# Cross-attention of a decoder layer: context sums behind the keys' norms, normed rows spread over a sequence, first queries turned before two value products

## The chip, the cores and the metric

The kernel runs on one core of one Trainium2 chip. The metric is the device time of one execution in microseconds (us); lower is better. The program's instructions are put into one queue for each engine ahead of time, by a planner that works with its own estimate of every duration; on the chip each queue runs in order, and an instruction starts when it is at the head of its queue and what it waits for has happened. Engine names in the profile: PE multiplies matrices (PEld loads its weights), DVE does vector work, ACT activations and copies, POOL general elementwise work, SP starts transfers.

## The reference, cut to what matters

Eight sequences of 112 tokens and width 512 pass one decoder layer: causal self-attention, cross-attention over 375 context rows for each sequence (32 heads of 16), and a mixture of eight experts (two for each token) plus a shared one. The change touches the cross-attention and the third layer norm behind it:

```python
x = x + attention(layernorm(x))
xn = layernorm(x)
q = rmsnorm((xn @ Wq.T).reshape(b, n, 32, 16))
kv = concat([ctx @ Wk.T, ctx @ Wv.T], -1).reshape(b, m, 32, 16, 2)
k, v = rmsnorm(kv[..., 0]), kv[..., 1]
x = x + softmax(q @ k.T * 16 ** -0.5) @ v
x = x + experts(layernorm(x))        # the third layer norm: xn3 in the kernel
```

## The kernel before, in words

**Stages.** Self-attention goes over four groups of heads, to about 423 us of the span. Then come the queries of all tokens and the first sequence's keys and values (423 to 482 us), then the loop of cross-attention over sequences b = 0 to 7 (482 to 742 us), and last the experts. All matrices are in 32-bit floats.

**Tokens.** They lie in seven tiles of 128 rows. Sequences 1 to 7 have the first 112 rows of a tile; sequence 0 is spread over the last 16 rows of all seven. So its queries need all seven tiles and are read with gaps.

**One pass of the loop.** For each half of the heads (`cp`) and each third of the context (`m`), `exp_scores` multiplies keys by queries (L816) into four PSUM tiles of the pool `sc`, and ACT takes the exponentials (L827). `weigh` multiplies the half that is pending by the values (L844, 96 small products). `attend(b - 2)` turns a finished tile and adds it to the rows. `produce` makes keys and values of sequence b + 1 in small portions. All other products (keys, values, `weigh`, every transpose) take their output from the pool `mm`, which has four tiles: a fifth product waits until an earlier one was read.

**Keys and values ahead.** The two first thirds of a context are multiplied with seven products in place of eight (`first_chunks`, L656). This needs four sums of context blocks, which POOL makes into the tiles `csum[0]` to `csum[3]` (`chunk_sums` and `block_sums`, L636 to L644). The first is read by the sixth product, the second by the second, the third by the fourth, the fourth by the seventh, and the result of the seventh is written to the values by DVE at L677. The third thirds of two neighbouring sequences are done together (`third_chunks`, with `pair_sums`, which writes `csum[0]`, `[1]`, `[4]` and `[2]`). So the same four tiles are written anew for every sequence. `chunk_sums(b)` is traced at the start of pass b - 1, but POOL may run it as soon as its tiles are free and its context is there; before, nothing else holds it.

**The boundary of two passes.** The squares of the last keys are made on POOL (L571) and summed on DVE (L572). `rms_scale_quick` takes reciprocal (DVE, L583) and square root (ACT, L584), with an activation table load on either side. `normed_k` (L787) then scales three thirds of the keys (DVE, L792, three instructions), turns them (PE, L797) and copies them (ACT, L800). `issue_after(last_exp[(b, 1, 2)])` puts these copies behind the last exponentials of the pass in ACT's queue. The next pass begins with an L816 product that is kept behind all that was traced on PE before it. `spread_q` (L775) makes the queries of a coming sequence in two DVE instructions (L779).

**The third layer norm.** `ln_apply` (L156) scales a tile's rows (DVE, L153, two buffers `xn`), turns them with four PE transposes (L160, output in `mm`) and copies them to `xn3` (ACT, L161). Tiles 0 to 3 are done at the boundary of passes 5 and 6, in this place:

```python
                if b == 5:
                    for t in range(4):
                        ln_apply(mv3, rs3, t, xn3)
```

They are first used in pass 7, by `shared_ahead` (L911).

**Before the loop.** Lines 890 to 899 give the order of the last steps: value product of the first third, keys of sequence 0, value product of the second third, `normed_q` of the last tile (L764: scaling, four transposes L772, copy L773), `spread_q(0)`, value product of the last third. Under `issue_after(squared)` POOL makes differences of weights (L627) and `chunk_sums(1)` beside these.

Of the kernel before, what the change touches and what calls it, by code (L numbers as in the profile page):

```python
# [18 lines left out]
ALU = mybir.AluOpType  # L19
# [57 lines left out]
def decoder_layer(  # L77
    ctx: ExitStack, tc: tile.TileContext, x, ctxT, wqk, wv_all, wo, wx, wgate, wsgu, wsd, wegu, wed_a, wed_b, consts, out
):
    nc = tc.nc  # L80
# [36 lines left out]
    def psum(pool, name):  # L117
        return pool.tile([P, 512], F32, tag=pool.name, name=name)
# [32 lines left out]
    def ln_normed(mv, rs, t):  # L151
        xn = lnpool.tile([P, D], F32, tag="xn", name="xn")
        nc.vector.tensor_scalar(xn, xs[t], mv[:, t, 0:1], rs[:, t : t + 1], ALU.subtract, ALU.mult)  # L153
        return xn

    def ln_apply(mv, rs, t, xnT):  # L156
        xn = ln_normed(mv, rs, t)
        pt = psum(mm, "ln_t")
        for c in range(ND):
            nc.tensor.transpose(pt[:, c * P : (c + 1) * P], xn[:, c * P : (c + 1) * P], ident)  # L160
        nc.scalar.copy(xnT[:, :, t * P : (t + 1) * P], pt.rearrange("p (c s) -> p c s", c=ND))  # L161
# [15 lines left out]
    with ExitStack() as sa:  # L177
# [120 lines left out]
        for g in range(NG):  # L298
# [226 lines left out]
            for i, b in enumerate(order):  # L525
# [10 lines left out]
                if b in (0, 6, 7):  # L536
                    t = max(b - 5, 0)
# [6 lines left out]
    mv3 = ln_begin("3")  # L544
    xn2 = xnpool.tile([P, ND, NT], F32, tag="xnT", name="xn2")
    xn3pool = ctx.enter_context(tc.tile_pool(name="normed3", bufs=1, side="right"))
    xn3 = xn3pool.tile([P, ND, NT], F32, name="xn3")
    with ExitStack() as xa:
# [11 lines left out]
        wxk, wxv, wxq = (load_w(wpool, wx[i], f"wx{i}") for i in range(3))  # L560
# [37 lines left out]
        def by_head(t):  # L598
            return t.rearrange("p (h d) -> p h d", h=XH)
# [15 lines left out]
        def project_v(b, m):  # L615
            nc.vector.tensor_copy(values[b % 2][:, m, :, :XD], by_head(project(b, m, wxv, "xv")))
# [12 lines left out]
        csum = [stp.tile([P, 2, MC], F32, name=f"csum{i}") for i in range(4)]  # L629
# [3 lines left out]
        def halves(b, m):  # L633
            return [ctxs[b][:, 2 * k : 2 * k + 2, m * MC : (m + 1) * MC] for k in range(2)]

        def block_sums(a11, a12, a21, a22, dst):  # L636

            nc.gpsimd.tensor_tensor(dst[0], a21, a22, ALU.add)
            nc.gpsimd.tensor_tensor(dst[1], dst[0], a11, ALU.subtract)
            nc.gpsimd.tensor_tensor(dst[2], a11, a21, ALU.subtract)  # L640
            nc.gpsimd.tensor_tensor(dst[3], a12, dst[1], ALU.subtract)

        def chunk_sums(b):
            block_sums(*halves(b, 0), *halves(b, 1), csum[:4])  # L644

        def pair_sums(b):
            block_sums(*halves(b, 2), *halves(b + 1, 2), [csum[0], csum[1], csum[4], csum[2]])
# [1 line left out]
        def product(x, w):  # L649
            ps = psum(mm, "kv")  # L650
            for c in range(2):
                nc.tensor.matmul(ps[:MC, :], x[:, c, :], w[:, c, :], start=(c == 0), stop=(c == 1))  # L652
            return ps[:MC, :]

        def first_chunks(b):

            (a11, a12), (a21, a22) = halves(b, 0), halves(b, 1)
            k0, k1 = rawk[b][0][:, 0, :], rawk[b][0][:, 1, :]
            v0, v1 = (values[b % 2][:, m, :, :XD] for m in range(2))
            u = stp.tile([MC, 512], F32, tag="u", name="u")  # L660
            nc.scalar.copy(k0, product(a11, wxk[:, 0:2]))
            yield
            nc.vector.tensor_tensor(u, product(csum[1], wt[1]), k0, ALU.add)
            yield
            nc.vector.tensor_tensor(k0, product(a12, wxk[:, 2:4]), k0, ALU.add)  # L665
            key_squares(b, 0)
            yield
            nc.vector.tensor_tensor(v1, by_head(product(csum[2], wt[2])), by_head(u), ALU.add)
            yield
            nc.vector.tensor_tensor(by_head(k1), by_head(product(a22, wt[3])), v1, ALU.add)  # L670
            key_squares(b, 1)
            yield
            p5 = product(csum[0], wt[0])
            nc.vector.tensor_tensor(v1, by_head(p5), v1, ALU.add)
            nc.vector.tensor_tensor(u, p5, u, ALU.add)
            yield
            nc.vector.tensor_tensor(v0, by_head(product(csum[3], wxv[:, 2:4])), by_head(u), ALU.add)  # L677
            yield

        def third_chunks(b):  # L680
# [32 lines left out]
        def produce(b, cp, m):  # L713

            if (cp, m) == (0, 0):
                new_keys(b)
                produce.first = first_chunks(b)
                if b > 1:
                    chunk_sums(b)
                if b + 1 < B:  # L720
                    ctxs[b + 1] = load_ctx(b + 1)
            first = produce.first
            if b == B - 1:
                if cp == 0:
                    steps(2, first)
                elif m == 0:
                    project_k(b, 2)
                elif m == 1:
                    project_v(b, 2)
                else:  # L730
                    steps(1, first)
            elif b % 2:
                if cp == 0:
                    steps(2, first)
                    if m == 2:
                        pair_sums(b)
                        produce.third = third_chunks(b)
                else:
                    if m == 1:
                        steps(1, first)  # L740
                    steps((2, 1, 2)[m], produce.third)
            else:
                if cp == 0 and m < 2:
                    steps(1, produce.third)
                steps(((0, 1, 2), (2, 1, 1))[cp][m], first)
# [29 lines left out]
        def spread_q(b):  # L775

            queries[b] = qtp.tile([P, ND, 2, S], F32, tag="qT2", name="qT2")
            for e in range(2):
                nc.vector.tensor_scalar(  # L779
                    like_seq(queries[b][:, :, e, :], b),  # L780
                    seq(xn2, b),
                    cst[:, C_EO + e : C_EO + e + 1],
                    None,
                    ALU.mult,
                )

        def normed_k(b):  # L787
            k, kss = rawk.pop(b)
            keys[b] = kvp.tile([P, ND, M], F32, tag="kT2", name="kT2")
            for m in range(NM):  # L790
                k3 = k[:, m, :].rearrange("p (h d) -> p h d", h=XH)
                nc.vector.tensor_tensor(  # L792
                    k3, k3, kss[:, m, :, None].to_broadcast([MC, XH, XD]), ALU.mult
                )
                pt = psum(mm, "kT")
                for c in range(ND):
                    nc.tensor.transpose(  # L797
                        pt[:, c * MC : (c + 1) * MC], k[:, m, c * P : (c + 1) * P], ident[:MC, :MC]
                    )
                nc.scalar.copy(  # L800
                    keys[b][:, :, m * MC : (m + 1) * MC],
                    pt[:, : ND * MC].rearrange("p (c s) -> p c s", c=ND),
                )
# [88 lines left out]
        project_v(0, 0)  # L892
        rms_scale(rawk[0][1].rearrange("p m h -> p (m h)"))
        normed_k(0)
        project_v(0, 1)
        normed_q(TT - 1)
        spread_q(0)
        project_v(0, 2)
        ctxs[1] = load_ctx(1)

# [5 lines left out]
        def shared_ahead(i, k):  # L906
# [6 lines left out]
                )  # L913
            nc.vector.tensor_copy(ahead[:, 2 * i + k, :HALF], ps[:, :HALF])

        pending = None
        for b in range(B):
            for cp in range(2):
                es = []
                for m in range(NM):  # L920
                    es.append(exp_scores(b, cp, m))
                    if m == 0 and pending is not None:
                        weigh(*pending)

                    if m == 1 and cp == 0 and b >= 2:
                        attend(b - 2)
                    if b + 1 < B:
                        produce(b + 1, cp, m)
                    elif m:
                        shared_ahead(cp, m - 1)  # L930
                pending = (b, cp, es)
            if b + 1 < B:
                spread_q(b + 1)

                with tc.issue_after(last_exp[(b, 1, 1)].ins):
                    if b == 5:
                        rs3 = ln_rstd(mv3, 0, 4)
                    rms_scale_quick(rawk[b + 1][1].rearrange("p m h -> p (m h)"))

                    tc.keep_in_program_order(nc.scalar.activation(warm, eps_rms[:1], AF.Exp))  # L940
                with tc.issue_after(last_exp[(b, 1, 2)].ins):
                    normed_k(b + 1)
                if b + 2 == B:
                    sw = [load_shared(i) for i in range(2)]
                    ahead = wpool.tile([P, 4, 512], F32, tag="w", name="ahead")
                if b == 5:
                    for t in range(4):
                        ln_apply(mv3, rs3, t, xn3)
        weigh(*pending)
        attend(TT - 1)  # L950

# [4 lines left out]
    with ExitStack() as ff:  # L956
# [190 lines left out]
        halves = (slice(0, SL), slice(SL, P))  # L1147
# [254 lines left out]
```

## Time and profile before

| what | value |
|---|---|
| median of 3 runs | 995.17 us (992.79 to 996.33) |
| the profiled execution | 994.56 us |
| its span (first to last instruction) | 992.7 us |
| granted TensorE clock, mean over the span | 0.997 |
| DVE, ACT, POOL busy | 44%, 30%, 36% of the span |

The profile shows one execution. Its span leaves 1.86 us outside. Starts are in us from the span's start. In a row of the timeline the number after the start is the duration of the whole row, and a bracket gives the idle time of the engine before it and what ended it. First products of the passes (L816) start at these times:

| pass b | 0 | 1 | 2 | 3 | 4 | 5 | 6 | 7 |
|---|---|---|---|---|---|---|---|---|
| start, us | 482.54 | 513.83 | 543.74 | 578.41 | 609.50 | 644.26 | 679.43 | 712.45 |

### The profile page before, as it was taken

To read this page: it belongs to the slowest core of one execution; us is meant where nothing else is said; L and a number is where in the kernel's file an instruction comes from. 1 tells how busy PE (TensorE), PEld (TensorE's weight loads), DVE (VectorE), ACT (ScalarE), POOL (GpSimd) and SP (SyncE) were. 2 spreads that over 40 slices of the span, in tenths; PEclk is the share of its full clock that TensorE was granted. 3 is DMA by queue.
4 is the path that set the end of the run, shared out by engine and by line. 5 is a ranking of instruction groups with operands and counts; after the bars stand their busy time and mean duration, and the time that the engine had idled before them with its cause. 6 is when DMAs were issued, how large, how long until landed. Compare 5 with 4: busy or idle time off the path is not lost.

```text
span 992.7 us, 16065 instructions
## 1 busy us (share of the span) xinstructions
PE 968.1 (98%) x6008; PEld 580.6 (58%) x6008; DVE 432.5 (44%) x885; ACT 302.7 (30%) x759; POOL 357.0 (36%) x408
## 2 busy tenths in 40 slices
PE   5999999999999999999999999999999999999998
PEld 3569756985598559845455555555665544444433
DVE  4346433542364236764445455544435143333324
ACT  3135102501151115224355355545542121111100
POOL 4337744683468444433523222321114600000023
PEclk9999999999999999999999999999999999999999
DMA  9522002201220121000010001100219648777755
GB/s 348 204 95 75 21 22 89 81 2 43 86 83 1 43 86 41 2 0 1 32 33 33 20 14 33 33 2 1 86 60 424 231 131 259 236 236 236 214 183 168
DMA packets 35324, 98.89 MB, mean 100 GB/s; under 512 B 4848, under 2 KB 10224, under 8 KB 31664
## 3 DMA queue, kind: packets, MB, share of 16 engines
q1 hardware_dynamic: 30192, 85.26, 25.7%
q0 software_dynamic: 2320, 7.63, 2.4%
q10 hardware_dynamic: 2736, 4.98, 1.7%
q8 instruction: 48, 0.79, 0.3%
q14 instruction: 28, 0.23, 0.1%
HBM read 78.85 MB, written 14.94 MB: 94 GB/s over the span
## 4 chain that ended last, share of the span: by engine, by line
PE 86%; DVE 4%; issue 4%; POOL 3%; DMA 2%; ACT 0%; POOLq 0%; SPq 0%; DVEq 0%; ACTq 0%
PE qk L274 16%; PE kv L652 12%; PE v L393 7%; PE o L473 7%; PE gu L972 5%; PE y L1230 5%; PE gate L1208 5%; PE up L1208 4%; PE xs L816 4%; PE pv L844 4%; PE z L230 3%; PE s L191 3%; PE o L432 1%; PE v L364 1%; POOL sq L571 1%
## 5 line engine op out<-in xcount | busy, mean ns | idle before, releaser
L827 ACT ACTIVATE e<-xs 125x448 f32<-125x448 f32 x192 | 88.4, 545 | 92.0 <-PE xs L816 92.0
L1241 POOL DMA_INDIRECT got<-routed,at x14 | 15.9, 1135 | 172.7 <-issue 172.4
L274 PE MATMUL qk<-xc,wc 128*128 128x448 f32 x180 | 70.1, 539 | 0.0
L652 PE MATMUL kv<-wx,ctx 128*125 128x512 f32 x120 | 56.7, 603 | 0.0
L211 ACT ACTIVATE s<-s,mx 112x112 f32<-112x112 f32 x128 | 48.1, 376 | 27.7 <-DVE mx L208 17.0
L1208 PE MATMUL gate<-wex,xT 128*64 x144 | 55.3, 466 | 0.5 <-ACT xT L1173 0.5
L972 PE MATMUL gu<-xn,sw 128*128 128x448 f32 x144 | 55.5, 541 | 0.0
L1208 PE MATMUL up<-wex,xT 128*64 x144 | 54.3, 459 | 0.0
L274 PEld LDWEIGHTS qk<-xc,wc 128*128 128x128 f32 x180 | 34.2, 190 | 33.5 <-issue 32.3
L1158 DVE COPY xn<-wex 128x704 f32 x60 | 31.2, 524 | 51.5 <-PE up L1208 51.5
L571 POOL TENSOR_TENSOR sq<-kraw 125x512 f32<-125x512 f32 x24 | 25.1, 1046 | 78.3 <-DVE kraw L665 20.5
L816 PEld LDWEIGHTS xs<-qT,kT 32*125 32x125 f32 x768 | 33.5, 183 | 32.6 <-issue 24.1
L816 PE MATMUL xs<-qT,kT 32*125 32x224 f32 x768 | 50.3, 374 | 1.5 <-DVE qT L779 1.5
L274 PE MATMUL qk<-xn,w 128*128 128x448 f32 x120 | 50.2, 539 | 0.0
L1230 PE MATMUL y<-wd,hT 128*64 128x512 f32 (+1 forms) x216 | 49.5, 592 | 0.6 <-ACT y L1234 0.6
L216 POOL TENSOR_TENSOR s<-s,sm 112x448 f32<-112x448 f32 x32 | 29.8, 932 | 49.5 <-DVE sm L215 45.0
L1208 PE MATMUL gate<-xn,xT 128*64 128x352 f32 x120 | 45.9, 464 | 0.0
L1208 PE MATMUL up<-xn,xT 128*64 128x352 f32 x120 | 45.3, 459 | 0.0
L972 PEld LDWEIGHTS gu<-xn,sw 128*128 128x128 f32 x144 | 26.8, 190 | 24.2 <-issue 24.2
L844 PE MATMUL pv<-e,v 125*32 125x112 f32 x1536 | 40.1, 260 | 0.2
L844 PEld LDWEIGHTS pv<-e,v 125*32 125x32 f32 x1536 | 36.3, 110 | 5.2 <-issue 3.2
L652 PE MATMUL kv<-wx,csum 128*125 128x512 f32 x80 | 38.9, 609 | 0.0
(274 smaller groups left out, 1965.5 us busy)
## 6 DMA issues: line engine op xcount, KB each, us to landing
wd<-in_wed_a SPq DMA_DIRECT2D x27, 512.0 KB, 3.8
wex<-in_wegu SPq DMA_DIRECT2D x8, 1408.0 KB, 19.2
wd<-in_wed_b SPq DMA_DIRECT2D x36, 192.0 KB, 4.5
w<-in_wqk SPq DMA_DIRECT2D x6, 1024.0 KB, 4.9
ctx<-in_ctxT SPq DMA_DIRECT2D x8, 750.0 KB, 4.3
slots<-zeros SPq DMA_DIRECT2D x1, 4608.0 KB, 20.0
wd<-in_wed_a SPq DMA_DIRECT2D x18, 256.0 KB, 4.4
routed<-y SPq DMA_DIRECT2D x18, 256.0 KB, 3.4
```

The source lines that it names most:

```text
L211: nc.scalar.activation(s[:, h, :], s[:, h, :], AF.Exp, bias=mx[:, h : h + 1], accum_out=sm[:, h : h + 1])
L274: nc.tensor.matmul(ps[:, :HALF], wt[:, c * P : (c + 1) * P], x[:, c, :], start=(c == 0), stop=(c == 1))
L393: nc.tensor.matmul(ps[:, :wide], x[:, c, cols], w[:, c, :], start=(c == 0), stop=(c == 1))
L473: nc.tensor.matmul(ps[:, :wide], x[:, h, :], w[:, h, :], start=(h == 0), stop=(h == 1))
L571: i = nc.gpsimd.tensor_tensor(sq[:n], dst, dst, ALU.mult)
L652: nc.tensor.matmul(ps[:MC, :], x[:, c, :], w[:, c, :], start=(c == 0), stop=(c == 1))
L816: i = nc.tensor.matmul(strips[j][:MC, ci * 2 * S : (ci + 1) * 2 * S], keys[b][rows, 2 * cp + ci, m * MC : (m + 1) * MC], queries[b][rows, ...
L827: last_exp[(b, cp, m)] = nc.scalar.activation(e[:, :, j, :, :].rearrange("p c e s -> p c (e s)"), strips[j][:MC, : 4 * S].rearrange("p (c ...
L844: nc.tensor.matmul(ps[VW * j : VW * (j + 1), g * S : (g + 1) * S], v[:, m, 16 * cp + h, :], es[m][:, h // 8, (h % 8) // 2, h % 2, :], star ...
L972: nc.tensor.matmul(ps[:, :HALF], w[:, c, i % 2, k, :], xn3[:, c, cols], start=(c == 0), stop=(c == ND - 1))
L1208: nc.tensor.matmul(gu[k][n, :FF], xT[:, c, n], w, start=(c == 0), stop=(c == ND - 1))
L1230: nc.tensor.matmul(ps[n, :], hT[:fn, i, n], w[i][:fn], start=(i == 0), stop=(i == len(FCH) - 1))
```

## The change

It has three edits. `block_sums` returns its four instructions, and for b > 1 `chunk_sums(b)` makes each of them wait for two DVE instructions that were traced last: the third L792 of `normed_k(b - 1)` and the L677 of `first_chunks(b - 1)`. `project_v(0, 1)` goes behind `normed_q(TT - 1)` and `spread_q(0)`. The four `ln_apply` calls leave the boundary of passes 5 and 6 and go into pass 6, one each behind `produce` of (cp, m) = (0, 1), (0, 2), (1, 1), (1, 2). The statistics `rs3` stay where they were.

```diff
         def chunk_sums(b):
-            block_sums(*halves(b, 0), *halves(b, 1), csum[:4])
+            sums = block_sums(*halves(b, 0), *halves(b, 1), csum[:4])
+            for i in sums if b > 1 else ():
+                for other in urgent.values():
+                    tc.add_manual_dep(
+                        i.ins, other.name, mybir.DependencyInfo(mybir.DependencyClass.Sync, mybir.DependencyReason.DATA)
+                    )
...
-            nc.vector.tensor_tensor(v0, by_head(product(csum[3], wxv[:, 2:4])), by_head(u), ALU.add)
+            i = nc.vector.tensor_tensor(v0, by_head(product(csum[3], wxv[:, 2:4])), by_head(u), ALU.add)
+            urgent["v"] = i.ins
...
-                nc.vector.tensor_tensor(
+                i = nc.vector.tensor_tensor(
                     k3, k3, kss[:, m, :, None].to_broadcast([MC, XH, XD]), ALU.mult
                 )
+                urgent["k"] = i.ins
...
-        project_v(0, 1)
         normed_q(TT - 1)
         spread_q(0)
+        project_v(0, 1)
         project_v(0, 2)
...
+        later_rows = ((0, 1), (0, 2), (1, 1), (1, 2))
...
                         produce(b + 1, cp, m)
+                        if b == 6 and (cp, m) in later_rows:
+                            ln_apply(mv3, rs3, later_rows.index((cp, m)), xn3)
...
-                if b == 5:
-                    for t in range(4):
-                        ln_apply(mv3, rs3, t, xn3)
```

More of the change, by code (lines that the diff above doesn't have):

```diff
@@ L636, in block_sums @@
         def block_sums(a11, a12, a21, a22, dst):
[L638 to L641, printed above, removed]
-        def chunk_sums(b):
-            block_sums(*halves(b, 0), *halves(b, 1), csum[:4])
+            return (
+                nc.gpsimd.tensor_tensor(dst[0], a21, a22, ALU.add),
+                nc.gpsimd.tensor_tensor(dst[1], dst[0], a11, ALU.subtract),
+                nc.gpsimd.tensor_tensor(dst[2], a11, a21, ALU.subtract),
+                nc.gpsimd.tensor_tensor(dst[3], a12, dst[1], ALU.subtract),
+            )
+        urgent = {}
+        def chunk_sums(b):
+            sums = block_sums(*halves(b, 0), *halves(b, 1), csum[:4])
[3 more added lines that the diff above has]
+                        i.ins, other.name, mybir.DependencyInfo(mybir.DependencyClass.Sync, mybir.DependencyReason.DATA)
+                    )
         def pair_sums(b):
```

## The prediction

> **What bounds the kernel now.** I read the page's busy shares first, then the chain of waits.
>
> ```profile
> PE 968.1 (98%) x6008; PEld 580.6 (58%) x6008; DVE 432.5 (44%) x885; ACT 302.7 (30%) x759; POOL 357.0 (36%) x408
> PE 86%; DVE 4%; issue 4%; POOL 3%; DMA 2%; ACT 0%; POOLq 0%; SPq 0%; DVEq 0%; ACTq 0%
> ```
>
> PE works through nearly all of the span, and the chain lies on it. So no edit here can win more than the gaps of PE that it closes, and every product moved to another place still costs its PE time there. I then looked, in the timeline, for gaps at the three places that the edits touch. The first is the start of the loop, by the chain of waits:
>
> ```profile
> 473.76 3.44 PE xv L589 x8
> ...
> 477.73 0.59 ACT xn L773
> ...
> 478.35 4.15 DVE qT L779 x2
> ...
> 482.54 1.04 PE xs L816 x16
> ```
>
> The last query tile is turned behind a value product, and DVE needs 4.15 us to spread the queries of sequence 0 (strided, with POOL's weight differences beside them). The last value product ends at 477.47 + 3.60 = 481.07; PE then idles 1.47 us by the timeline.
>
> The second is the boundary into pass 2, by the timeline:
>
> ```profile
> 539.63 0.72 POOL L640 TENSOR_TENSOR csum<-ctx,ctx 128x250 f32<-128x250 f32 x1 [2.28 <-DMA ctx<-in_ctxT]
> 540.16 2.85 DVE L792 TENSOR_TENSOR kraw<-kraw,kss 125x512 f32<-125x512 f32 x3
> 540.31 1.07 POOL L638 TENSOR_TENSOR csum<-ctx 128x250 f32<-128x250 f32 x1
> ...
> 541.44 1.79 ACT L827 ACTIVATE e<-xs 125x448 f32<-125x448 f32 x4
> ...
> 543.07 0.65 PE L797 MATMUL kT<-cst,kraw 125*128 125x125 f32 x4 [0.44 <-DVE kraw L792]
> 543.14 1.49 ACT L800 COPY kT<-kT 128x500 f32<-128x500 f32 x3
> 543.74 0.69 PEld L816 LDWEIGHTS xs<-qT,kT 32*125 32x125 f32 x16 [0.25 <-ACT kT L800]
> ```
>
> Three L792 take 2.85 us while POOL's sums run beside them. At the boundary into pass 6, where the first two have no sum beside them, three take 1.89. The last row matters most: the weights of the first score product were released by ACT's copy of the turned keys, not by DVE.
>
> The third is the boundary into pass 6, by the timeline, and then the table of stretches (length; busy us and instructions of PE, PEld, DVE, ACT, POOL; granted clock; DMA):
>
> ```profile
> 672.41 1.68 PE L797 MATMUL kT<-cst,kraw 125*128 125x125 f32 x12
> ...
> 674.58 1.49 ACT L800 COPY kT<-kT 128x500 f32<-128x500 f32 x3
> ...
> 676.05 3.45 PE L160 MATMUL ln_t<-cst,xn 128*128 128x128 f32 x16 [1.95 <-DVE v L677]
> ...
> 679.43 1.22 PE L816 MATMUL xs<-qT,kT 32*125 32x224 f32 x16
> ```
>
> ```profile
> 676.00:678.00 2.00, 1.95 (x10) 1.70 (x11) 0.83 (x2) 0.94 (x3) 0.00 (x0) 0.61 0.00 0
> 678.00:679.40 1.40, 1.40 (x8) 0.96 (x6) 0.27 (x1) 0.89 (x2) 0.00 (x0) 0.50 0.00 0
> ```
>
> PE idles 1.95 us until L677 has freed an `mm` tile, and then turns four row tiles in 3.45 us at about half the granted clock.
>
> **Edit 1, the queries sooner.** The four transposes of the last tile now follow the keys' twelve. Their rows are scaled by 471.53 + 1.29 = 472.82, and PE is through with the keys at about 473.6, so they run to about 474.1. ACT's three key copies end at 472.95 + 1.53 = 474.48, the query copy (0.58) near 475.1. The spread (4.15, POOL is busy beside it in both places) ends near 479.3. PE has two value products of 3.60 us from 474.1 and ends them at 481.1 as before, 1.8 us after the spread. The score product then starts at 481.1 in place of 482.54: **-1.4 us**. DVE's copies of the two value products queue behind the spread, but `weigh` wants them only at 497. If the spread grew by more than 1.8 us the gain would shrink; its bounds are 0 and 1.47. SP's load of context 2 waits for the last value product and goes out at 481.1 in both.
>
> **Edit 2, the sums held.** For b = 2, 4, 6 nothing moves: before the boundary into pass 1, say, the last L792 is over at 510.5 and the first sum starts at 510.99. For b = 3, 5, 7 the sums now start behind L677.
>
> Into pass 2, the three keys' turns would come up to 1 us earlier, but ACT's exponentials end at 541.44 + 1.79 = 543.23 and the copies are queued behind them. The first copy still ends near 543.7 and the product still starts at 543.74. What is left is `weigh`: 544.82 against 543.74 + 0.97 (sixteen score products, from 513.83 to 514.80 in pass 1): 0.1 us. The exponentials hang on the square root and two table loads, which the sums don't touch.
>
> Into pass 4, three L792 take 3.30 us, and the third turn starts at 608.93. Without sums L638 and L639 it would start near 608.0 (L640 of the pair is not held and still delays the first). ACT's exponentials end at 606.85 + 1.79 = 608.64, the first copy near 609.1, the product near 609.15 in place of 609.50. L677 ends at 610.62 before and delays `weigh` by another 0.2. Together 0.55 us.
>
> Into pass 6 nothing on the path hangs on a sum. Edit 2: **-0.65 us**.
>
> Here a rule is weighed. The Trainium skill, "SBUF — State Buffer", section "Who interferes with whom", says that a DVE instruction with two SBUF inputs and a POOL instruction that reads SBUF shut each other out for whole instructions. The rows agree (0.62 for L638 alone, 1.07 beside L792). By the rule alone, each held sum returns its full wait: (2.85 - 1.89) + (3.30 - 1.89) for L792 and twice (1.23 - 0.80) for L779, 3.2 us. The same section adds that PE and ACT never wait on anyone for these ports, and here ACT is late next. I take 0.65 and keep 0 and 3.2 as ends.
>
> The added wait: behind the sums in POOL's queue stand the copy L856 (553.01 before) and the squares of the next keys (556.15). PE asks for `csum[1]` at 549.08. From the end of L677 (544.77) two sums of 0.63 and 0.67 are ready at 546.1: 3.0 us of cover. The others are asked for at 554.5 and later. Cost zero while POOL takes them at once.
>
> **Edit 3, the rows spread.** At the boundary into pass 6 PE is through with the keys at 672.41 + 1.68 = 674.1. Next late is again ACT: exponentials to 672.89 + 1.79 = 674.68, first copy to about 675.15, product at 675.2. After 0.97 us `weigh` starts at 676.17; L677 ended at 675.99 with two L153 ahead of it, so it doesn't bind. Before, `weigh` started at 680.58: 4.4 us less. In pass 6 come sixteen transposes. Four of them hold PE for 0.44 us where it is busy (start 451.40, next product 451.84), so 4 x 0.44 = 1.8 us. The Trainium skill, "TensorE: Matmul & The Clock Gate", section "Back-to-back issue gap", would have 81 ns for each, 1.3 us; the row is of these very transposes, and I take it. DVE gets four L153 of 0.55, ACT four copies of 0.58 in a pass in which they are busy 13.35 and 16.55 of 33.0 us, and PE 33.0: hidden, if they are ready in time. Edit 3: -4.4 + 1.8 = **-2.6 us**. Ends: -4.4 (transposes fall into gaps) and +3.8 (below).
>
> On the clock, that page's section "The HAM clock gate (the "warmup" mystery)" asks for an idle window of about 3.4 us before the clock halves. Here 1.95 us of idling went before 0.61 and 0.50, while the 1.47 us at 481 left it at 1.00. By the rule the dip isn't the gap's doing and could come again: some 2 us for 3.4 us at half speed. By the row it goes, since 1.1 us of gap is left. I take the row.
>
> **Sum.** 1.4 + 0.65 + 2.6 = 4.65 us. Behind the loop all loads start by what the loop frees, so they move along. The profiled execution took 994.56 (span 992.7 and 1.86 around): 989.9. It lay 0.6 below the median of 995.17, which would give 990.5. I say 990.2.
>
> **Rivals.**
> *The held time comes back in full* (3.2 us in place of 0.65): 990.2 - 2.5 = 987.7. For it: PE waits for L792 in four rows, 1.5 us. Against: ACT's copies.
> *Part is lost*: the clock dips again (2 us), or the spread eats edit 1 (1.4): 992 to 994. For it: the free clock above. Against: 1.8 us of cover.
> *The rows stall PE*: in pass 6 the transposes stand in PE's queue and wait for L153, which stands on DVE behind the consumers of the products just before. By their rows (0.2 to start, 0.69 for a consumer, two of them in the second place, 0.55 for L153) this is 1.45 + 2.1 + 1.45 + 1.45 = 6.4 us. Edit 3 becomes -4.4 + 1.8 + 6.4 = +3.8, the sum -1.4 - 0.65 + 3.8 = +1.75: 996.6 on the footing of 990.2, slower than before. It decides from 1.2 us for each of the four. Against: L153 needs only `rs3` and a free `xn`, and DVE is busy 13.35 us of 33.0 in pass 6, so it should run early.
> *The sums sink in POOL's queue* behind L856: `csum[1]` at 553.3 + 1.3 = 554.6 against 549.08, three times 5.5 us: 1006. Against: L856 becomes ready 8 us later than they do.
>
> **How the numbers follow.** About 0.3% (3 us) is what a measurement tells from no change. Forecast 0.56 (988.4 to 992.0); full return 0.11; part lost 0.17, two thirds of it within 3 us; rows stall 0.11, half of it slower by over 3 us, since the waits are only bounded; sums sink 0.05. Faster: 0.56 + 0.11 + 0.05 = 0.72 at most, 0.70 with some scatter; slower 0.11; within 0.19. Range 987.2 to 995.2: it takes in the first three cases and the noise of 1.8 us about the median.
>
> **What would show it.** First product of pass 0 near 481.1 with no idle time before it; of pass 2 still released by ACT; L792 near 1.9 to 2.4 us for three; no wait of PE for L677 into pass 6 and a clock of 1.00 there; pass 6 longer by about 1.8 us plus the head it gained (some 4), and no PE wait on L153. Wrong: a PE wait for `csum`, or pass 6 more than 4 us longer from its `weigh` on.

## The result, and the profile after

| | before | changed |
|---|---|---|
| median | 994.57 us (992.79 to 996.33, 7 runs) | 990.82 us (989.13 to 991.68, 7 runs) |
| profiled execution | 994.56 us, span 992.7 | 989.52 us, span 987.7 |
| granted clock over the span | 0.997 | 0.999 |

The ratio of changed to before is 0.9961 (95% interval 0.9949 to 0.9972): 3.9 us faster, between 2.8 and 5.1. Timed again beside later experiments, it was 0.9963 (0.9949 to 0.9976). The predicted 990.2 lies 0.6 us under the median. One of the 62 executions of the kernel before that were timed beside the experiments took 2039 us and is left out of all that follows. Line numbers move by the change: the score product L816 is now L828, its exponentials L839, the key scalings L803, the key turns L809 and their copies L812, the last value addition L687, the sums L639 to L642.

The busy shares of the page and the engines' shares of the chain after:

```profile
PE 965.8 (98%) x6008; PEld 579.8 (59%) x6008; DVE 427.2 (43%) x885; ACT 302.3 (31%) x759; POOL 353.9 (36%) x408
PE 87%; issue 4%; ACT 3%; POOL 3%; DVE 2%; DMA 2%; SPq 0%; POOLq 0%; DVEq 0%; ACTq 0%
```

DVE and ACT have changed places in the chain (DVE 4% to 2%, ACT 0% to 3%). That is the first sign of what holds PE up next. The start of the loop, by the chain of waits after:

```profile
472.32 1.28 PE kT L809 x12
473.60 0.44 PE qT L783 x4
474.04 6.87 PE xv L589 x16
480.91 0.97 PE xs L828 x16
```

The turn of the last queries stands directly behind the keys' turns, two value products cover the spread, and the score product follows with no wait.

The boundary into pass 2, by the timeline after:

```profile
538.09 0.72 POOL L641 TENSOR_TENSOR csum<-ctx,ctx 128x250 f32<-128x250 f32 x1 [2.44 <-DMA ctx<-in_ctxT]
...
538.46 2.11 DVE L803 TENSOR_TENSOR kraw<-kraw,kss 125x512 f32<-125x512 f32 x3
539.45 1.81 PE L809 MATMUL kT<-cst,kraw 125*128 125x125 f32 x12
...
539.74 1.79 ACT L839 ACTIVATE e<-xs 125x448 f32<-125x448 f32 x4
...
541.43 1.49 ACT L812 COPY kT<-kT 128x500 f32<-128x500 f32 x3
541.97 0.63 POOL L639 TENSOR_TENSOR csum<-ctx 128x250 f32<-128x250 f32 x1 [3.15 <-DVE v L687]
542.04 1.04 PE L828 MATMUL xs<-qT,kT 32*125 32x224 f32 x16 [0.78 <-ACT kT L812]
```

Three scalings take 2.11 us in place of 2.85 and the keys' turns run as one row. But PE now stands still for 0.78 us, and the bracket names ACT's copy, which follows the exponentials (539.74 + 1.79 = 541.53; the two rows overlap by 0.1). The three scalings are above 1.89 because the first still overlaps the pair's sum at 538.09, which is not held. The held sum starts when L687 is through. The boundary into pass 6, by the timeline after, with its first `weigh` products, and the stretches around it:

```profile
670.04 1.68 PE L809 MATMUL kT<-cst,kraw 125*128 125x125 f32 x12
...
672.21 1.48 ACT L812 COPY kT<-kT 128x500 f32<-128x500 f32 x3
...
672.82 1.04 PE L828 MATMUL xs<-qT,kT 32*125 32x224 f32 x16 [1.09 <-ACT kT L812]
673.78 2.51 PE L856 MATMUL pv<-e,v 125*32 125x112 f32 x96
```

```profile
671.70:672.80 1.10, 0.03 (x1) 0.00 (x0) 1.10 (x4) 1.10 (x4) 0.00 (x0) 1.00 0.00 0
672.80:675.00 2.20, 2.18 (x68) 1.90 (x72) 0.46 (x1) 2.03 (x5) 1.66 (x3) 1.00 0.00 0
```

The 1.95 us of idling and the 3.45 us of transposes are gone from here (the transposes are now in pass 6); 1.09 us of waiting for ACT is left, and the clock stays at 1.00.

The starts of the passes (first score product) give a length for each. "Head" is from the keys' first turn to pass 0; pass 7 counts to the end of the span. "Loop" is the sum, from the keys' first turn to the end:

| us | first turn at | head | 0 | 1 | 2 | 3 | 4 | 5 | 6 | 7 and experts | loop |
|---|---|---|---|---|---|---|---|---|---|---|---|
| before | 472.32 | 10.22 | 31.29 | 29.91 | 34.67 | 31.09 | 34.76 | 35.17 | 33.02 | 280.25 | 520.38 |
| changed | 472.15 | 8.69 | 31.29 | 29.91 | 34.56 | 30.73 | 34.56 | 30.93 | 34.59 | 280.29 | 515.55 |

The boundary *into* pass b counts to the length of pass b - 1, up to its first product; a wait of `weigh` behind that product counts to pass b. Of the 5.0 us between the two spans 0.17 lies ahead of the first turn, where nothing was changed; 4.83 is in the loop.

### The profile page after: what moved, and what is told of

It reads as the page before. It is cut to its first block, busy times and chain, and to the rows that moved or that the text cites. A ratio compares the mean times of both kernels' runs of the same rounds, so it can differ in the third digit from the quotient of the medians.

```text
span 987.7 us, 16063 instructions
## 1 busy us (share of the span) xinstructions
PE 965.8 (98%) x6008; PEld 579.8 (59%) x6008; DVE 427.2 (43%) x885; ACT 302.3 (31%) x759; POOL 353.9 (36%) x408
## 4 chain that ended last, share of the span: by engine, by line
PE 87%; issue 4%; ACT 3%; POOL 3%; DVE 2%; DMA 2%; SPq 0%; POOLq 0%; DVEq 0%; ACTq 0%
PE qk L274 16%; PE kv L662 12%; PE v L393 7%; PE o L473 7%; PE gu L985 5%; PE y L1243 5%; PE gate L1221 5%; PE xs L828 4%; PE up L1221 4%; PE pv L856 4%; PE z L230 3%; PE s L191 3%; PE o L432 1%; PE xv L589 1%; PE v L364 1%
## 5 line engine op out<-in xcount | busy, mean ns | idle before, releaser
L839 ACT ACTIVATE e<-xs 125x448 f32<-125x448 f32 x192 | 88.4, 545 | 87.6 <-PE xs L828 87.6
L828 PE MATMUL xs<-qT,kT 32*125 32x224 f32 x768 | 50.1, 373 | 2.7 <-ACT kT L812 2.7
L828 PEld LDWEIGHTS xs<-qT,kT 32*125 32x125 f32 x768 | 33.3, 181 | 32.0 <-issue 23.3
```

Source lines behind the costliest of these rows:

```text
L828: i = nc.tensor.matmul(strips[j][:MC, ci * 2 * S : (ci + 1) * 2 * S], keys[b][rows, 2 * cp + ci, m * MC : (m + 1) * MC], queries[b][rows, ...
L839: last_exp[(b, cp, m)] = nc.scalar.activation(e[:, :, j, :, :].rearrange("p c e s -> p c (e s)"), strips[j][:MC, : 4 * S].rearrange("p (c ...
```

## The experiments

The column "first turn at" matters for all that follows: it was 472.0 to 472.3 in three profiled executions and 473.8 to 474.2 in six, whatever the kernel. So the spans of single profiles are not compared below; the loop is.

### Each edit alone, and two without the hold

**e1_queries** has the kernel before with this edit only:

```diff
-        project_v(0, 1)
         normed_q(TT - 1)
         spread_q(0)
+        project_v(0, 1)
```

> Only edit 1 (the second value product behind the turn and spread of the first queries). Theory (PE idled 1.47 us there and nothing else): the first score product of pass 0 starts 1.4 to 1.5 us sooner after the keys' turns, all later stages keep their lengths (pass 2 34.67, pass 4 34.76, pass 5 35.17 us), span 1.5 us shorter, some 991.2. Rival (the gain is given back later, because contexts and sums move too): some later pass is longer by as much, span 992.7.

**e2_hold** is the changed kernel with the order of `project_v` and the place of the four `ln_apply` put back; only the sums are held.

> Only edit 2 (the sums held). Theory (behind the contention ACT is late next): three key scalings fall to 1.9 to 2.2 us, but into pass 2 the score product keeps its place and only weigh comes 0.1 us sooner, into pass 4 weigh 0.55 us sooner; into pass 6, where the four row tiles stay at the boundary, L677 comes up to 0.35 us sooner and the row turns with it. Span shorter by 0.65 to 1.0 us. Rival (each contended microsecond comes back): 3.2 us shorter. It also shows whether the clock dips again into pass 6 when PE idles some 1.6 us in place of 1.95.

**e3_rows** has only the four `ln_apply` in pass 6 (the order of `project_v` is put back in it), and **e13_no_hold** is the changed kernel with no wait for the sums; both have

```diff
-            for i in sums if b > 1 else ():
+            for i in ():
```

> Only edit 3 (the rows spread over pass 6). Theory: pass 5 to 6 boundary loses 4.2 us (1.95 of idling, the transposes at the low clock), pass 6 is 1.6 to 1.8 us longer, span 2.6 us shorter, clock 1.00 at the boundary. Rival (the saving hangs on the held sums, since a sum beside the row scalings delays L677 and with it weigh): the boundary loses under 3.5 us and weigh waits for L677.

> Edits 1 and 3 without the hold. Theory: the gains add, span 4.2 us shorter than before and 0.5 to 0.8 longer than with all three. Rival (contention comes back in full): 2 us or more longer than with all three.

| us | head | 2 | 3 | 4 | 5 | 6 | loop | ratio to before (95% interval) |
|---|---|---|---|---|---|---|---|---|
| before | 10.22 | 34.67 | 31.09 | 34.76 | 35.17 | 33.02 | 520.38 | |
| e1_queries | 8.68 | 34.76 | 30.74 | 34.73 | 35.04 | 33.54 | 518.93 | 0.9991 (0.9980 to 1.0001) |
| e2_hold | 10.23 | 34.55 | 30.74 | 34.56 | 34.47 | 32.84 | 519.14 | 0.9998 (0.9988 to 1.0008) |
| e3_rows | 10.22 | 34.77 | 31.00 | 34.76 | 30.93 | 34.59 | 517.53 | 0.9976 (0.9967 to 0.9984) |
| e13_no_hold | 8.68 | 34.71 | 30.74 | 34.71 | 30.92 | 34.59 | 515.92 | 0.9953 (0.9936 to 0.9969) |
| changed | 8.69 | 34.56 | 30.73 | 34.56 | 30.93 | 34.59 | 515.55 | 0.9961 (0.9949 to 0.9972) |

**Edit 1** takes 1.54 us from the head with nothing of it given back there. One thing was not expected: pass 3 is 0.35 us shorter too, without any hold. In this execution the sum of the pair started 0.47 us before the key scalings (605.53 against 606.00), before it was 0.09 (605.48 against 605.57), so it delayed the first scaling less. In e3_rows, which has neither edit 1 nor the hold, the lead was 0.17 us and the pass took 31.00; in e13_no_hold 0.49 us and 30.74. So without the hold the length of pass 3 hangs on when the pair's sum runs; that edit 1 is what moves that sum is not shown. Pass 6 is longer by 0.52; the clock dipped into it, as before.

**Edit 3** takes 4.24 us from the end of pass 5 and adds 1.57 to pass 6, 2.7 us together, with or without the hold. L687 ran later without it (676.79 to 677.47 in e3_rows), but `weigh` still started 0.97 us behind the score product (677.63), 0.16 us after L687's end. The rival that the saving hangs on the held sums is refuted.

**Edit 2** alone has a loop shorter by 1.24 us than the profile of before, more than expected and far from 3.2. Passes 2 to 4 give 0.67 of it, the boundary into pass 6 gives 0.70 and 0.18 behind it, and the experts' stage took 0.30 more in this execution. The timed executions do not bear the gain out: the ratio of 0.9998 is 0.2 us, and by its interval at most 1.2. The profile of before had a dip of the clock into pass 6, which e2_hold does not have and which many executions of before do not have either (see edit 3 in the next section). And the hold has a price of its own there, as the timeline of e2_hold shows:

```profile
676.57 1.09 PE L160 MATMUL ln_t<-cst,xn 128*128 128x128 f32 x8 [1.59 <-DVE v L687]
...
677.26 1.65 DVE L153 TENSOR_SCALAR xn<-x,mv,rs 128x512 f32<-128x512 f32 x2 [0.75 <-PE ln_t L160]
...
678.24 0.63 PE L160 MATMUL ln_t<-cst,xn 128*128 128x128 f32 x4 [0.58 <-DVE xn L153]
```

The held sums run here from 676.59 on, beside the last two row scalings, which take 1.65 us in place of twice 0.55 before, and PE waits for them, 0.58 and then 0.19 us. With edit 3 the rows are no longer there, so neither the gain nor the price into pass 6 is left. What the hold adds to the other two edits is the difference between e13_no_hold and the changed kernel: 515.92 - 515.55 = 0.37 us, 0.15 in each of passes 2 and 4. That is below what the timed runs can see; their intervals overlap widely. Why it is so little is seen in the timeline of e13_no_hold into pass 2:

```profile
540.18 2.89 DVE L803 TENSOR_TENSOR kraw<-kraw,kss 125x512 f32<-125x512 f32 x3
540.36 1.08 POOL L639 TENSOR_TENSOR csum<-ctx 128x250 f32<-128x250 f32 x1
...
541.47 1.79 ACT L839 ACTIVATE e<-xs 125x448 f32<-125x448 f32 x4
...
543.16 1.48 ACT L812 COPY kT<-kT 128x500 f32<-128x500 f32 x3
543.76 0.69 PEld L828 LDWEIGHTS xs<-qT,kT 32*125 32x125 f32 x16 [0.22 <-ACT kT L812]
```

The scalings are held up in full, 2.89 us. Yet from ACT's exponentials (541.47) to the score product it is 2.29 us here, and 2.30 us in the changed kernel (539.74 to 542.04). ACT sets the time in both; the hold only turns time in which PE waited for DVE into time in which it waits for ACT.

### The cover of the hold

**e6_longer_hold** makes the sums wait for one instruction more, DVE's copy of the `weigh` product:

```diff
-            nc.vector.tensor_copy(
+            i = nc.vector.tensor_copy(
                 turned[b][:, cp, :, :S], ps[:, : 4 * S].rearrange("p (g s) -> p g s", g=4)
             )
+            urgent["w"] = i.ins
```

> The changed kernel with the sums held longer: also behind DVE's copy of the weigh product that runs at the start of the pass. Theory (cover of the hold: csum[1] ready at 543.8, asked for at 547.3 into pass 2, so 3.4 us): the first sum starts near 546.2, the third in POOL's order, csum[1], is ready near 548.1, PE waits 0.8 to 1.0 us for a sum in passes 2, 4 and 6, span 2.4 to 3.0 us longer. Rival (another cover exists, the products asked for later can absorb it): no change within 0.3 us.

The loop took 518.33 us, 2.8 more than the changed kernel; passes 2, 4 and 6 took 35.57, 35.58 and 35.61, 1.0 more each. The timeline of e6_longer_hold in pass 2:

```profile
548.20 0.63 POOL L639 TENSOR_TENSOR csum<-ctx 128x250 f32<-128x250 f32 x1 [7.59 <-DVE oT L871]
548.79 0.63 POOL L641 TENSOR_TENSOR csum<-ctx 128x250 f32<-128x250 f32 x1
549.37 0.67 POOL L640 TENSOR_TENSOR csum<-csum,ctx 128x250 f32<-128x250 f32 x1
...
550.10 1.98 PE L662 MATMUL kv<-wt,csum 128*125 128x512 f32 x4 [0.75 <-POOL csum L640]
```

The copy, the last that the sums wait for, ends 4.4 us after L687 does (548.12 against 543.69), and the product starts 1.0 us late. Nothing absorbs it: the pass grows by as much. The cover of the hold is the 3.4 us that the expectation reckoned, and the rival of a deeper cover is refuted. The ratio to before was 0.9989 (0.9981 to 0.9997): most of the change's gain is gone.

### Filling the gap that ACT leaves

If ACT is late next, PE's idle time there can be used. **e7_fill** puts the first product for the next keys ahead of the first score product of passes 2, 4 and 6, and queues the query spread and the row scalings behind L687:

```diff
+            if b and b % 2 == 0:
+                new_keys(b + 1)
+                produce.first = first_chunks(b + 1)
+                steps(1, produce.first)
             for cp in range(2):
...
-                spread_q(b + 1)
+                with tc.issue_after(last_value[b]) if b else nullcontext():
+                    spread_q(b + 1)
...
-                            ln_apply(mv3, rs3, later_rows.index((cp, m)), xn3)
+                            with tc.issue_after(last_value[6]):
+                                ln_apply(mv3, rs3, later_rows.index((cp, m)), xn3)
```

(`last_value[b]` is the L687 of `first_chunks(b)`; `produce` takes one step less at its old place.)

> The changed kernel, with the gap filled that ACT leaves at the boundaries into passes 2, 4 and 6: the first product of the next keys (L662, 1.9 us of PE) is put ahead of the first score product there, and the query spreads and row scalings are queued behind L687 on DVE, so that its PSUM tile is free sooner. Theory (ACT's exponentials and copies are late next, and PE idles 0.78, 0.85 and 1.09 us for them): the product starts within 0.3 us of the keys' turns, the waits for ACT go, loop 2.0 to 2.7 us shorter than with the change. Rival (DVE, not ACT, sets the boundary, or the wait only moves to the product's own copy): loop the same within 0.3 us.

It took 988.18 us (986.81 to 989.71, 6 runs), ratio to before 0.9943 (0.9928 to 0.9958), and its loop 512.97 us: 2.6 less than with the change (2.5 less than the one measured beside it). The changed kernel, measured beside it:

> The changed kernel again, as the footing of the two beside it. Theory: the loop from the keys' first turn to the end takes 515.5 us within 0.2; what differs between executions is the stretch before it (472.15 us in the profile of after, some 1.7 us more in the profiles of the four single edits).

It took 990.98 us (989.29 to 991.50, 6 runs), its loop 515.43 us, its first turn was at 473.86. The timeline of e7_fill into pass 2:

```profile
539.32 1.73 PE L811 MATMUL kT<-cst,kraw 125*128 125x125 f32 x12
...
540.27 0.68 DVE L687 TENSOR_TENSOR v<-kv,u 125x512 f32<-125x512 f32 x1
...
541.00 1.98 PE L662 MATMUL kv<-wx,ctx 128*125 128x512 f32 x4
541.31 1.49 ACT L814 COPY kT<-kT 128x500 f32<-128x500 f32 x3
...
542.91 1.04 PE L830 MATMUL xs<-qT,kT 32*125 32x224 f32 x16
```

L687 comes directly behind the key scalings and frees the product's PSUM tile at 540.95; the product fills the gap, and the first third of the keys is copied at 541.86, 1.05 us before the score product. None of PE's waits for ACT's key copies is left. This is the strongest evidence for the reading of the boundaries: PE waited 2.7 us for ACT in the changed kernel (0.78 + 0.85 + 1.09), and 2.5 to 2.6 us came back. Two things were changed at once, the place of the product and the order on DVE that frees its PSUM tile in time; the second alone was not tried. It is also the fastest kernel of the study.

## Why the prediction was right, step by step

**Edit 1** was put at -1.4 us, up to 1.47. The head lost 1.53 in the changed kernel and 1.54 alone, just above the bound. Timed alone it is 0.9 us, with an interval from -0.1 to 2.0. The spread of the first queries together with the next sequence's, before and after:

```profile
478.35 4.87 DVE L779 TENSOR_SCALAR qT<-xn,cst 128x448 f32<-128x448 f32 x4 [0.42 <-ACT xn L773]
```

```profile
474.84 3.18 DVE L790 TENSOR_SCALAR qT<-xn,cst 128x448 f32<-128x448 f32 x4 [1.57 <-ACT xn L784]
```

It took 3.18 us at its new place, against 4.87, so the cover was larger than reckoned.

**Edit 2** was put at -0.65. Beside the other two edits it is worth 0.37 by the loop. The mechanism held into pass 2: the score product into pass 2 was released by ACT as before, and `weigh` came 0.1 us sooner. The term that was mis-sized is the 0.35 us of the score product into pass 4. It came with edit 1 alone as well, when the pair's sum, which waits for a context to land, ran a little earlier. The rule of the Trainium skill that was weighed ("SBUF — State Buffer", section "Who interferes with whom": exclusive use of the shared ports) agrees with the instructions here (a sum takes 0.63 us alone and 1.08 beside the scalings), and taken as a sum it would have been off by nearly 3 us: the runs show that DVE's wait was not the one that ended last. The full-return rival falls with e13_no_hold.

**Edit 3** was put at -4.4 + 1.8. `weigh` started in pass 6 of the kernel before with this row:

```profile
680.58 2.51 PE L844 MATMUL pv<-e,v 125*32 125x112 f32 x96
```

Its start moved by 6.80 us (to 673.78), of which 1.70 is the shift at the start of pass 0 and 0.67 the passes between: 4.43. From that `weigh` to pass 7 it is 33.63 us in place of 31.87, 1.76 for sixteen transposes, as four times 0.44 had it. The sign given for pass 6, longer by 1.8 us "plus the head it gained", was a slip: the 4 us ahead of its first product belong to pass 5, which shrank by 4.24, and pass 6 grew by 1.57.

A term that falls short is the clock. I took the row, in which 1.95 us of idling went before the dip, and wrote that the dip goes. It went: none of the 13 timed executions of the changed kernel has a clock under 0.999. But it was not always there: of the 61 executions of before that ran beside the experiments, 37 have a clock of 0.997 or 0.998 and 24 have 0.999. The spans of each kernel fall into two groups (see the last section), and sorted by both they read:

| spans, us (executions) | short group | long group |
|---|---|---|
| before, clock 0.997 or 0.998 | 991.7 to 992.6 (19) | 993.8 to 995.2 (18) |
| before, clock 0.999 | 990.8 to 991.4 (5) | 992.4 to 993.5 (19) |
| changed | 987.3 to 987.7 (4) | 989.0 to 989.9 (9) |

By the medians of these groups the change is worth 4.8 to 4.9 us against executions with the dip and 3.4 to 3.5 us against those without; the dip itself costs 1.3 to 1.5 us. The profiled execution had it, so its 4.4 us are those of an execution with it, and the timed ratio (3.9 us) lies between the two kinds. The Trainium skill, "TensorE: Matmul & The Clock Gate", section "The HAM clock gate (the "warmup" mystery)", says that the activity window runs freely. A dip in some executions and not in others fits that better than the reading in the prediction, in which 1.95 us always brings it; the page's window of about 3.4 us, though, is longer than this gap. Whether the gap was as long in the executions without a dip is not known, since none of them was profiled. The rival in which the rows stall PE did not come true: PE has no wait for a row scaling in pass 6.

**The sinking sums** did not come true either, but e6_longer_hold shows what a late sum costs: 1 us of cover too little is 1 us in each of three passes. The working of the 3.0 us of cover left out a sum: three come before `csum[1]` is ready (with L641 between), not two, since the hold also takes L641 back from its early place (533.86 before, there as L640). That L687 ends some 1.2 us sooner against the start of the pass (541.89 against 542.04, before 544.77 against 543.74) more than made up for it.

**The sum** of 4.65 us stands beside 4.83 in the loop. Edits 1 and 3 brought 0.2 more than put down together (1.53 and 4.43 - 1.76 = 2.67). Passes 2 to 4 are 0.67 us shorter, as put down for edit 2, but some 0.3 of it need not be the hold's. For the executions without a dip the sum is about 1.2 us too high, and against the timed 3.9 it is 0.75 too high. The footing of 994.85 that the 990.2 stands on is 0.3 above the median of all seven runs, which offsets a part. So the mechanisms of edits 1 and 3 were right, and that the number came so near is in part luck.

## What to carry to other kernels

When two engines stand in each other's way, ask first which wait ends last behind both of them: the releaser of PE's next instruction told here, in one row, that 3.2 us of contention were worth under 0.7 (0.37 by the loops). A stall of PE is worth more filled than shortened: moving the row turns out of the boundary and a product into it brought 2.7 and 2.6 us by the profiled loops, though the first includes a dip that not every execution had. And look for what an instruction waits for besides its data; here the transposes waited for a PSUM tile that an instruction behind four others on DVE was to free.

## What was not expected of the hardware

**The start of the span.** The first sixteen products of the first projection (L332) took 6.28 us in the profiles of before, changed and e7_fill, and 7.87 to 8.37 in the six others. The rows of the chain of waits of the changed kernel, and then of e1_queries:

```profile
14.32 6.28 PE qk L332 x16
```

```profile
14.39 8.37 PE qk L332 x16
```

The slowest of these products took 0.64 us in the one case and 1.12 in the other. One by one, the first six of e1_queries start 0.74 to 0.91 us apart, and from the eighth on 0.38; in the changed kernel all but the first are 0.38 apart. The transposes before them (L160) start 0.21 us apart in both, later ones 0.11. So the pace doubles within a product or two, as it would at twice the clock, but the table of stretches shows a clock of 1.00 in all these stretches. What held the products back is therefore not shown by any run here. The 1.6 to 2.1 us fit the two groups into which the timed spans of a kernel fall: for the changed kernel four spans of 987.3 to 987.7 and nine of 989.0 to 989.9, with none between. In all nine profiled executions the short first products go with a first turn at 472.0 to 472.3, the long ones with 473.8 to 474.2.

**The clock behind a gap.** The dip into pass 6 followed an idle time of 1.95 us in before and again in e1_queries (clocks of 0.60 and 0.55 in the two stretches of 2 us from 677), not one of 1.59 us (e2_hold) or 1.09 us (changed). In all 12 timed executions of e1_queries the clock over the span was 0.997 or 0.998, and in the 12 of e2_hold 0.999 or more. The dip does not begin at the gap's end in e1_queries: the first eight transposes behind it, from 676.10, took 1.09 us, as they did in e2_hold without a dip, and the clock of the stretch up to 677 is 1.00. The gap is also not the whole of the stretch: from the keys' first turn to the score product of pass 6 PE only turns and idles, for 7.02 us in before, 6.89 in e1_queries, 6.32 in e2_hold and 2.78 in the changed kernel. That e1_queries dips and e2_hold does not can come from the 0.36 us of idling, from the length of this stretch or from where it lies in time; which of these decides was not tried. The gap's length alone does not, if the gap of before was the same in its 24 executions without a dip.
